# A fifth block product of the first layer, the fourth, taken by seven products of its own blocks

## The chip, the cores and the metric

The kernel runs on one core of one Trainium2 chip. The metric is the device time of one execution, in microseconds (us), as a median of several runs. All data are 32-bit floats.

## What is computed

Each of 4096 tokens of 512 numbers first passes a quaternion rotation (one 4x4 mixing of its four quarters of 128), then a mixture of 8 experts. Each token goes to the two experts that score highest, and an expert takes 1024 slots. Cut to what matters here, for expert e:

```python
h  = relu(de @ fc1_w[e].T + fc1_b[e])   # first layer:  1024 slots x 512 -> 2048
eo = h @ fc2_w[e] + fc2_b[e]            # second layer: 1024 slots x 2048 -> 512
out = x + sum(gates * eo[slot])         # rows go back to their tokens, weighted
```

## The kernel before, in words

TensorE (PE) does the matrix products into PSUM banks of 128 x 512 floats. VectorE (DVE) and ScalarE (ACT) read the banks and add into tiles of SBUF. GpSimd (POOL) forms the sums of weight blocks, gathers and scatters rows. SyncE (SP) issues the other transfers.

**Groups.** The work goes by 32 groups k = 4e + g: expert e, quarter g of its 2048 hidden units (512 of them). In a group each layer is a 2 x 2 by 2 x 2 block product, done with seven block products in place of eight (Strassen's method in Winograd's form); the sums of blocks that this needs are made by POOL for weights (`left1`, `right2`, `left_sub`, lines 110 to 162) and by POOL and DVE for inputs (`factors`, `right_sub`).

**First layer** (`layer1`, from line 842). One block product is 256 hidden units x 256 inputs x 512 slots. Taken whole, as `half` does it for products 0, 5 and 4, it is four matmuls of 128 x 512. Products 1, 6, 3 and 2 are instead taken by seven products of their own blocks (128 x 128 x 256 slots), each one matmul (`within`, line 831, which writes half a bank). Products 1 and 6 go together, as do 3 and 2 (`pair`, line 874): the left half of a bank is the term of the one and the right half that of the other, so a matmul pair (`both`) is followed by one DVE add that reads the whole bank (L888, L901, L907). Bank `t` accumulates term after term and is read in between; term 4 goes to another bank, `u`. The results are four tiles of 128 x 2 x 512: `h11`, `h21`, `r12`, which lie side by side in `beside`, and `h22`. Product 4 belongs to two of them: its value is added to `h21`'s running value to give `h22` (L925), and to `r12` (L917).

**Second layer** (`second_layers`). One of its units is a block product in four matmuls of 128 x 256 (`product2`, L796) and one add on DVE into the expert's accumulator (L1160, L1164, L1186, L1188, L1209, L1216, L1132).

**Each fp32 matmul is two instruction records on PE in the profile.** So a group has 112 records on L796, 24 of width 512 on L854 and 56 on L833.

**Order.** Two generators, first and second layer, are run in turn: one unit of the first, one unit of the second, 14 of each in a group; the first layer is two units ahead of the second's group. In between, `turn` takes steps from two lists: `background` (steps of rotating the next expert's rows on DVE and ACT, L723, L765, L767, the sums between layers of `chain`, and the stores) and `fetches` (gathers on POOL, exchanges on SP). The table `PACE` says how many steps follow each unit. `later` puts the sums of blocks after chosen units. The instructions of an engine run in the order in which they are written, and the framework sets the waits.

**PSUM.** `bank1` hands out four banks in rotation to the first layer: `a0`, `a1`, `t`, `u`, `b0`, `b1`, `t`, `u`. The second layer has three, the rotation one.

Of the kernel before, what the change touches and what calls it, by code (L numbers as in the profile page):

```python
# [39 lines left out]
P = 128  # L40
# [11 lines left out]
NG = 4  # L52
# [14 lines left out]
def kernel(  # L67
# [509 lines left out]
    hp = ctx.enter_context(tc.tile_pool(name="hp", bufs=1))  # L577
    vp = ctx.enter_context(tc.tile_pool(name="vp", bufs=3))
    xdp = ctx.enter_context(tc.tile_pool(name="xdp", bufs=2))
# [33 lines left out]

    beside = [hp.tile([P, 3, 2, HALF], F32, name=f"beside{i}") for i in range(2)]
    unused = [hp.tile([P, 2, HALF], F32, name=f"hidden{i}") for i in range(5)]

# [55 lines left out]
    class Slots:  # L672
# [36 lines left out]

        def arrivals(self, half):  # L710

            n = PER if half == 0 else 2
            t = self.a if half == 0 else self.b
            for at in range(0, PER, n):
                for st in range(n):
                    yield lambda st=st, at=at: self.gather_ahead(t[:, st], half, at + st)
                yield from [lambda: None] * 2
                for b in range(QT):
                    yield lambda b=b, at=at: self.exchange(t, half, at, b)
                yield from [lambda: None] * 2  # L720

# [70 lines left out]
    def product2(out, st0, factors, n, first, tiles=range(2)):  # L792

        for m in tiles:
            for c in range(2):
                nc.tensor.matmul(  # L796
                    out[m] if isinstance(out, list) else out[:, m],
                    lhsT=factors[0][n][:, c, (st0 + m) * P : (st0 + m + 1) * P],
                    rhs=factors[1][n][:, c, :],
                    start=first and c == 0 and (m == 0 or isinstance(out, list)),  # L800
                    stop=c == 1,
                    skip_group_check=True,
                )
        if st0 + 2 == PER and 1 in tiles and n in (2, 3, 4, 5):
            unused.append(factors[0][n])

    def chain(k, h22):


        h11, h21, r12 = (beside[k % 2][:, i] for i in range(3))  # L810
        s1, s2 = unused.pop(0), unused.pop(0)
        hidden[k] = [h11, h21, None, h22, s1, s2, r12]

        def last():
# [6 lines left out]
            lambda: V.scalar_tensor_tensor(r12, r12, 0.0, h11, ALU.max, ALU.subtract),  # L821
            *[lambda: None] * (2 if k == NK - 1 else 0),
            last,
        ]

    hidden = {}

    def relu(h):
        nc.scalar.activation(h, h, AF.Relu)  # L829
# [12 lines left out]
    def layer1(k, factors, subs):  # L842
# [4 lines left out]
        h = beside[k % 2]  # L847
        h11, h21, r12 = (h[:, i] for i in range(3))
        A, B = slice(0, HS), slice(HS, HALF)
# [23 lines left out]

        def pair(n, o, at, base, base_read):

            two = h[:, at : at + 2]
            t, u = bank1(f"t{n}_{k}"), bank1(f"u{n}_{k}")
            halves = t.rearrange("p (n s) -> p n s", n=2)  # L880

            def both(bank, i, first=False):
                within(bank[:, A], subs, n, i, first)
                within(bank[:, B], subs, o, i)

            def add(m, half):
                to = two[:, :, m, half]
                V.tensor_tensor(to, halves, to, ALU.add)  # L888

            within(base[:, A], subs, o, 1)  # L890
            within(base[:, B], subs, o, 2)
            base_read()
            both(t, 0, True)
            add(0, A)
            yield
            both(t, 5)
            add(0, B)
            both(u, 4, True)
            to = two[:, :, :, B]
            term = u.rearrange("p (n s) -> p n s", n=2).unsqueeze(2).to_broadcast([P, 2, 2, HS])  # L900
            V.tensor_tensor(to, term, to, ALU.add)  # L901
            yield
            both(t, 6)
            add(1, B)
            within(u[:, A], subs, n, 1, True)
            within(u[:, B], subs, n, 2)
            V.tensor_tensor(two[:, 0, 0], u, two[:, 0, 0], ALU.add)  # L907
            yield
            both(t, 3)
            add(1, A)  # L910
            relu(two[:, 0])

        def from5(m):
            nc.scalar.activation(h21[:, m], a[m], AF.Identity, bias=hi[:, m : m + 1])

        def from4(m):
            V.tensor_tensor(r12[:, m], b[m], r12[:, m], ALU.add)  # L917

        yield from pair(1, 6, 0, a[0], lambda: from5(0))
        yield  # L920
        h22 = unused.pop(0)
        b = [bank1(f"b{m}_{k}") for m in range(2)]
        for m in range(2):
            half(b[m], m, 4, True)
            V.tensor_tensor(h22[:, m], b[m], h21[:, m], ALU.add)  # L925
            if m == 1:
                from4(1)
                relu(h22)
            yield
        yield from pair(3, 2, 1, b[0], lambda: from4(0))  # L930
        chain(k, h22)
        yield

    PAIRS = (slice(0, 2 * P), slice(2 * P, 4 * P))

    def layer1_plain(k, w, x):
# [3 lines left out]

        h11, h21, r12 = (beside[k % 2][:, i] for i in range(3))
        h22 = unused.pop(0)
        for half in range(2):
# [6 lines left out]
            for at, i in ((at, i) for at in parts for i in range(NJ)):  # L950
# [22 lines left out]
                if half == 1 and done:  # L973
                    chain(k, h22)
                if len(parts) == 1 or i % 2:
                    yield

    def first_layers():
# [42 lines left out]
        lefts, right_subs = {}, {}  # L1021
        TURN_OF_SUM = {8: 2, 9: 0, 10: 1, 13: 3}
        nxt = None
        for k in range(NK):
            e, g = divmod(k, NG)
# [26 lines left out]
            if k:  # L1052
                for n, block, turns in (
                    (2, left_f[2], (2, 2, 3, 3)),
                    (3, w1_of[k][:, 1, 1], (4, 4, 5, 5)),
                ):
                    lefts[n], more = left_sub(k, n, block)
                    later(more, turns)
                if k == 1 or g == 0:
                    for n, turns in ((6, (1, 2, 2, 3)), (2, (4, 4, 5, 5)), (3, (6, 7, 8, 9))):  # L1060
                        right_subs[n], more = right_sub(xtp, e, n, xf[n])
                        later(more, turns)
# [6 lines left out]
            for i, _ in enumerate(units):  # L1069
# [3 lines left out]
                if k:  # L1073

                    if i == 8 and k + 1 < NK:
                        lefts[6], more = left_sub(k + 1, 6, left_n[6])
                        later(more, (9, 10, 11, 12))
                        lefts[1], more = left_sub(k + 1, 1, w1_of[k + 1][:, 0, 1])
                        later(more, (10, 11, 12, 13))
                        if g == NG - 1:  # L1080
                            right_subs[1], more = right_sub(xtp, e + 1, 1, xf_n[1])
                            later(more, (8, 9, 9, 12))
                    for f in ahead[i]:
                        f()
# [8 lines left out]
                if e + 1 < E:  # L1093

                    if (g, i) in ((0, 12 if e else 5), (1, 8)):
                        fetches.extend(nxt.arrivals(g))
                    if (g, i) in ((1, 11), (2, 9)):
                        background.extend(nxt.steps(g - 1))
# [21 lines left out]
    def second_layers():  # L1120
# [17 lines left out]
        for n, (k, st0) in enumerate(units):  # L1138
# [22 lines left out]
            yield  # L1161
            v2 = vp.tile([P, 2, DB], F32, tag="v", name=f"v2_{k}_{st0}")
            product2(a, st0, factors, 5, False)
            V.tensor_tensor(v2, a, i12, ALU.add)  # L1164
            yield
            tiles = STORED[2 * st0 : 2 * st0 + 4]
            last = n + 1 == len(units)
            if last:
# [4 lines left out]
                for m in range(2):  # L1173
                    r.weigh(tiles[m], o11[:, m], LEFT)
                    r.weigh(tiles[m], v2[:, m], RIGHT)
                    r.weigh(tiles[2 + m], i21[:, m], LEFT)
# [6 lines left out]
            yield  # L1183
            v3 = vp.tile([P, 2, DB], F32, tag="v", name=f"v3_{k}_{st0}")
            product2(a, st0, factors, 6, False)
            V.tensor_tensor(v3, a, i22, ALU.add)  # L1186
            for m in range(2) if last else [slice(0, 2)]:
                V.tensor_tensor(o22[:, m], b[m] if last else b, v3[:, m], ALU.add)  # L1188
            yield
# [25 lines left out]
            product2(b, st0, factors, 2, False)  # L1215
            V.tensor_tensor(o12, b, v2, ALU.add)  # L1216
            if last_of_group and k + 1 < NK:
# [12 lines left out]
    PACE = (  # L1230
        [(1, 1)] * 2 + [(0, 1)] * 4 + [(0, 0)] + [(0, 1)] * 5 + [(1, 1), (0, 0)],
        [(1, 1)] * 4 + [(1, 1), (0, 2), (0, 0), (0, 1), (1, 1)] + [(0, 1)] * 3 + [(1, 1), (0, 0)],
        [(1, 1)] * 2 + [(2, 1)] * 2 + [(1, 2), (0, 2), (0, 0), (0, 1), (1, 1)]
        + [(0, 1)] * 3 + [(1, 1), (0, 0)],
    )

    with tc.manual_schedule():
# [5 lines left out]
        while going:  # L1243
            going = False
            for n, gen in enumerate((first, second)):
# [3 lines left out]
                k, i = now  # L1249
                turn(1 if k in (0, NK - 1) else PACE[0 if k == 1 else min(k % NG, 2)][i][n])  # L1250
        while background:
# [46 lines left out]
```

## Time and profile before

| | |
|---|---|
| median of 3 runs | 1569.85 us (1569.73 to 1571.15) |
| the profiled execution's own time | 1569.29 us |
| its span, first to last instruction | 1567.4 us |
| PEld (weight loads), busy | 1190.9 us (76%) |
| ACT busy | 318.9 us (20%), 450 instructions |
| POOL busy | 1048.7 us (67%), 1133 instructions |
| granted TensorE clock | 0.987 on the mean |

The profile is one execution, seen by the hardware profiler. A row of groups gives line, engine, operation, tiles (output<-inputs), shape and count; then busy time and mean ns of one; then idle time of the engine before them, and what ended it. A row of the timeline gives start and length in us, then the same, and in brackets the idle time before it with its releaser. Matmul ends are modelled and overlap the next start, so the pace of PE is read from starts. In a group's 46.5 us in the middle of the run (700 to 746.5) PE is busy for 46.38 us, DVE for 39.00, ACT for 9.60 and POOL for 23.98.

### The profile page before, as it was taken

How to read it: one execution, taken by the hardware profiler on the slowest of the kernel's cores; microseconds unless marked ns; L12 is line 12 of the kernel's file. 1: busy time of each engine (PE TensorE's matmuls, PEld its weight loads, DVE VectorE, ACT ScalarE, POOL GpSimd, SP SyncE). 2: the span in 40 equal slices, each digit the busy share in tenths (PEclk: the TensorE clock that was granted, in tenths of full speed). 3: DMA queues.
4: the chain of work that ended last, by engine and by line, in shares of the span. 5: the costliest groups of instructions: out<-in, count | busy, mean ns of one | idle time of the engine just before them, and what ended most of it. 6: DMA issues, size and time to landing. Idle time of an engine off the chain costs nothing.

```text
span 1567.4 us, 17504 instructions
## 1 busy us (share of the span) xinstructions
PE 1529.9 (98%) x6399; PEld 1190.9 (76%) x6399; DVE 1152.7 (74%) x1601; ACT 318.9 (20%) x450; POOL 1048.7 (67%) x1133
## 2 busy tenths in 40 slices
PE   5899999999999999999999999999999999999996
PEld 3677877877777787777887777787787787777785
DVE  6568886588856887578875888758886688866665
ACT  3222112221122112222112221122113121221110
POOL 1754687746977477965779468775697747794535
PEclk7899999999999999999999999999999999999998
DMA  8463123511334103531135311342133420331003
GB/s 324 160 212 94 55 68 117 140 59 55 113 97 139 62 28 114 148 116 55 33 104 159 93 55 61 121 123 79 55 102 102 139 64 28 114 107 54 11 17 106
DMA packets 79373, 152.18 MB, mean 97 GB/s; under 512 B 12022, under 2 KB 40950, under 8 KB 74168
## 3 DMA queue, kind: packets, MB, share of 16 engines
q1 hardware_dynamic: 56848, 90.24, 18.7%
q0 software_dynamic: 18048, 52.31, 10.8%
q10 hardware_dynamic: 4392, 8.52, 1.4%
q8 instruction: 50, 0.82, 0.2%
q14 instruction: 35, 0.29, 0.1%
HBM read 119.77 MB, written 25.23 MB: 93 GB/s over the span
## 4 chain that ended last, share of the span: by engine, by line
PE 91%; DVE 4%; issue 2%; DMA 2%; POOL 1%; SPq 0%; POOLq 0%; DVEq 0%
PE a L796 26%; PE b L796 20%; PE t L833 14%; PE a L854 12%; PE u L833 7%; PE b L854 7%; PE p L955 2%; PE b L833 2%; PE a L833 1%; DMA xb<-in_xt_dram 1%; DVE hidden L820 1%; DVE xa L767 1%; POOL rows L601 0%; DVE hidden L816 0%; POOL out_dram L657 0%
## 5 line engine op out<-in xcount | busy, mean ns | idle before, releaser
L796 PE MATMUL a<-t,hidden 128*128 128x256 f32 x1024 | 244.0, 382 | 5.3 <-DVE v L1186 5.2
L796 PEld LDWEIGHTS a<-t,hidden 128*128 128x128 f32 x1024 | 195.9, 191 | 58.5 <-issue 27.5
L888 DVE TENSOR_TENSOR beside<-t,beside 128x512 f32<-128x512 f32 x248 | 170.3, 687 | 94.3 <-PE t L833 90.4
L829 ACT ACTIVATE beside<-beside 128x1024 f32<-128x1024 f32 x62 | 65.5, 1057 | 558.0 <-DVE beside L888 558.0
L833 PE MATMUL t<-xsub,sub 128*128 128x256 f32 x496 | 127.9, 380 | 0.4
L796 PEld LDWEIGHTS b<-w,hidden 128*128 128x128 f32 x504 | 96.0, 190 | 38.9 <-issue 29.1
L796 PE MATMUL b<-w,beside 128*128 128x256 f32 x512 | 121.1, 380 | 0.6 <-DVE acc L1209 0.6
L796 PE MATMUL a<-t,beside 128*128 128x256 f32 x512 | 121.0, 379 | 0.0
L796 PE MATMUL a<-w,beside 128*128 128x256 f32 x512 | 121.0, 379 | 0.0
L796 PE MATMUL b<-t,hidden 128*128 128x256 f32 x504 | 119.1, 379 | 0.0
L796 PE MATMUL b<-w,hidden 128*128 128x256 f32 x504 | 119.1, 379 | 0.0
L796 PEld LDWEIGHTS b<-w,beside 128*128 128x128 f32 x512 | 97.4, 190 | 27.1 <-issue 15.7
L796 PEld LDWEIGHTS a<-w,beside 128*128 128x128 f32 x512 | 97.5, 190 | 26.2 <-issue 14.8
L854 PE MATMUL b<-x,s 128*128 128x512 f32 x248 | 116.6, 593 | 0.0
L854 PE MATMUL a<-x,s 128*128 128x512 f32 x248 | 116.6, 593 | 0.0
L854 PE MATMUL a<-xa,w 128*128 128x512 f32 x248 | 116.4, 593 | 0.0
L137 POOL TENSOR_TENSOR s<-w 128x512 f32<-128x512 f32 x31 | 39.5, 1274 | 112.7 <-PE b L854 112.7
L139 POOL TENSOR_TENSOR s<-w 128x512 f32<-128x512 f32 x31 | 39.8, 1283 | 111.3 <-PE t L833 111.3
L140 POOL TENSOR_TENSOR s<-w,s 128x512 f32<-128x512 f32 x31 | 39.4, 1270 | 107.5 <-PE t L833 101.9
L796 PEld LDWEIGHTS a<-t,beside 128*128 128x128 f32 x512 | 97.4, 190 | 13.1
L796 PEld LDWEIGHTS b<-t,hidden 128*128 128x128 f32 x504 | 96.0, 190 | 12.8
L833 PEld LDWEIGHTS t<-xsub,sub 128*128 128x128 f32 x496 | 94.0, 190 | 14.6 <-DVE beside L888 2.3
(233 smaller groups left out, 3089.4 us busy)
## 6 DMA issues: line engine op xcount, KB each, us to landing
w<-in_w_dram SPq DMA_DIRECT2D x64, 1024.0 KB, 5.1
xb<-in_xt_dram SPq DMA_DIRECT2D x8, 1024.0 KB, 9.9
out_dram<-in_x_dram ACTq DMA_DIRECT2D x1, 8192.0 KB
rows<-xa SPq DMA_DIRECT2D x112, 64.0 KB, 2.1
rows<-xb SPq DMA_DIRECT2D x224, 32.0 KB, 1.9
b<-in_b_dram POOLq DMA_DIRECT2D x8, 256.0 KB, 3.8
c<-choice,slot_cho POOLq DMA_INDIRECT x64, 2.3
rows<-out_dram,slot_tok POOLq DMA_INDIRECT x64, 3.5
```

The source lines that it names most:

```text
L137: lambda: G.tensor_tensor(s[0], w[:, 1, 0], w[:, 1, 1], ALU.add),
L139: lambda: G.tensor_tensor(s[2], w[:, 0, 0], w[:, 1, 0], ALU.subtract),
L140: lambda: G.tensor_tensor(s[3], w[:, 0, 1], s[1], ALU.subtract),
L767: V.scalar_tensor_tensor(to, t, M[:, i, j : j + 1], to, ALU.mult, ALU.add)
L796: nc.tensor.matmul(out[m] if isinstance(out, list) else out[:, m], lhsT=factors[0][n][:, c, (st0 + m) * P : (st0 + m + 1) * P], rhs=factor ...
L820: lambda: V.tensor_tensor(s2, s1, h11, ALU.subtract),
L829: nc.scalar.activation(h, h, AF.Relu)
L833: nc.tensor.matmul(out, lhsT=subs[0][n][i], rhs=subs[1][n][i], start=first, stop=True, skip_group_check=True,)
L854: nc.tensor.matmul(out, lhsT=factors[0][n][:, c, m * P : (m + 1) * P], rhs=factors[1][n][:, c, :], start=first and c == 0, stop=c == 1, sk ...
L888: V.tensor_tensor(to, halves, to, ALU.add)
L955: nc.tensor.matmul(ps[n][m][:, at], lhsT=w[:, block, i // 2, i % 2, m * P : (m + 1) * P], rhs=x.of(half, i)[:, at], start=i == 0 and at.st ...
```

## The change

Product 4 of the first layer is taken by seven products of its own blocks, in all 31 groups that `layer1` does. Lines here are those of the changed kernel, where `within`'s matmul is L836.

- The two products without a sum of inputs, 1 and 2, go side by side into bank `b` (`singles`) and are added to `h21` for the first half of `h22` (L929); ACT copies `h21`'s second half to `h22` first (L925).
- The other five terms, 0, 5, 4, 6 and 3, go to one bank, `t4`: 0, 5, 6 and 3 accumulate in its left half, 4 is made in its right half. Each is added to both `h22` and `r12` by one DVE instruction, whose PSUM operand is repeated (`add_to_both`, L897; term 4 by L938).
- `h22` moves into `beside`, between `h11` and `h21`; the first layer's banks of a group are then `a0`, `a1`, `t`, `u`, `b`, `t4`, `t`, `u`.
- POOL forms four more sums of weight blocks a group (`left_sub` for 4), DVE four more of inputs an expert (`right_sub` for 4).
- The last sum of `chain` (s4) now waits in a list until product 2 of the group before has freed its tile. `v2` and `v3` of the second layer are gone: their adds write into the accumulator. The steps of gathering, exchanging, rotating and summing are placed after other units (`ARRIVE`, `PACE`, `later`).

The units of the first layer in a group stay 14. The core of the diff:

```diff
-    beside = [hp.tile([P, 3, 2, HALF], F32, name=f"beside{i}") for i in range(2)]
-    unused = [hp.tile([P, 2, HALF], F32, name=f"hidden{i}") for i in range(5)]
+    beside = [hp.tile([P, 4, 2, HALF], F32, name=f"beside{i}") for i in range(2)]
+    unused = [hp.tile([P, 2, HALF], F32, name=f"hidden{i}") for i in range(3)]
...
-        b = [bank1(f"b{m}_{k}") for m in range(2)]
-        for m in range(2):
-            half(b[m], m, 4, True)
-            V.tensor_tensor(h22[:, m], b[m], h21[:, m], ALU.add)
-            if m == 1:
-                from4(1)
-                relu(h22)
-            yield
-        yield from pair(3, 2, 1, b[0], lambda: from4(0))
-        chain(k, h22)
+        def add_to_both(two, m, half, term):
+
+            to = two[:, :, m, half]
+            V.tensor_tensor(to, term.unsqueeze(1).to_broadcast([P, 2, HS]), to, ALU.add)
...
+        nc.scalar.activation(h22[:, 1], h21[:, 1], AF.Copy)
+        two = h[:, 1:4:2]
+        b, t4 = bank1(f"b_{k}"), bank1(f"t4_{k}")
+        singles(b, 4, True)
+        V.tensor_tensor(h22[:, 0], b, h21[:, 0], ALU.add)
+        within(t4[:, A], subs, 4, 0, True)
+        add_to_both(two, 0, A, t4[:, A])
+        yield
+        within(t4[:, A], subs, 4, 5)
+        add_to_both(two, 0, B, t4[:, A])
+        within(t4[:, B], subs, 4, 4)
+        to = two[:, :, :, B]
+        term = t4[:, B].unsqueeze(1).unsqueeze(1).to_broadcast([P, 2, 2, HS])
+        V.tensor_tensor(to, term, to, ALU.add)
+        yield
+        three = h[:, 2:4]
+        t, u = bank1(f"t3_{k}"), bank1(f"u3_{k}")
+        singles(b, 2)
+        within(t4[:, A], subs, 4, 6)
+        add_to_both(two, 1, B, t4[:, A])
+        both(t, 3, 2, 0, True)
+        add_pair(r12, b)
+        add(three, 0, A, t)
+        yield
+        within(t4[:, A], subs, 4, 3)
+        add_to_both(two, 1, A, t4[:, A])
+        relu(h22)
+        both(t, 3, 2, 5)
...
                 for n, block, turns in (
-                    (2, left_f[2], (2, 2, 3, 3)),
-                    (3, w1_of[k][:, 1, 1], (4, 4, 5, 5)),
+                    (4, left_f[4], (2, 2, 3, 3)),
+                    (2, left_f[2], (4, 4, 5, 5)),
+                    (3, w1_of[k][:, 1, 1], (6, 6, 7, 7)),
                 ):
...
-                    for n, turns in ((6, (1, 2, 2, 3)), (2, (4, 4, 5, 5)), (3, (6, 7, 8, 9))):
+                    for n, turns in (
+                        (6, (2, 2, 3, 3)),
+                        (4, (3, 4, 4, 5)),
+                        (2, (5, 7, 7, 8)),
+                        (3, (8, 10, 10, 12)),
+                    ):
...
-            v2 = vp.tile([P, 2, DB], F32, tag="v", name=f"v2_{k}_{st0}")
             product2(a, st0, factors, 5, False)
-            V.tensor_tensor(v2, a, i12, ALU.add)
+            V.tensor_tensor(o12, a, i12, ALU.add)
```

`add` (L887), `add_twice` (L892) and `add_pair` (L900) are `pair`'s adds under names of their own. In the changed kernel the first add of the second layer's product 3 is L1266 (before: L1209), its start's L1191 (before: L1132).

## The prediction

> **What bounds the kernel now.** I read the page first, then the groups with shapes kept apart, then the timeline of two stretches. The page:
>
> ```profile
> span 1567.4 us, 17504 instructions
> ...
> PE 1529.9 (98%) x6399; PEld 1190.9 (76%) x6399; DVE 1152.7 (74%) x1601; ACT 318.9 (20%) x450; POOL 1048.7 (67%) x1133
> ...
> PE   5899999999999999999999999999999999999996
> ...
> PE 91%; DVE 4%; issue 2%; DMA 2%; POOL 1%; SPq 0%; POOLq 0%; DVEq 0%
> ```
>
> PE is full in all but the first and last slices and holds 91% of the chain that ended last. No other engine has to be waited for in between: what PE is spared comes off the time, and what PE is made to wait is added to it, whole. The groups say how full:
>
> ```profile
> L888 DVE TENSOR_TENSOR beside<-t,beside 128x512 f32<-128x512 f32 x248 | 170.3, 687 | 94.3 <-PE t L833 90.4 <-ACT beside L914 1.7
> L833 PE MATMUL t<-xsub,sub 128*128 128x256 f32 x496 | 127.9, 380 | 0.4
> ...
> L854 PE MATMUL b<-x,s 128*128 128x512 f32 x248 | 116.6, 593 | 0.0
> ...
> L901 DVE TENSOR_TENSOR beside<-u,beside 128x1024 f32<-128x1024 f32 x62 | 75.9, 1225 | 9.5 <-PE u L833 7.3
> ...
> L170 DVE TENSOR_TENSOR xsub<-x 128x256 f32<-128x256 f32 x16 | 14.2, 886 | 0.0
> ...
> L170 DVE TENSOR_TENSOR xsub<-xb 128x256 f32<-128x256 f32 x8 | 3.3, 415 | 0.0
> ```
>
> The matmuls have next to no idle time in front; DVE waits for PE, not the reverse. Means of matmuls overlap, so I take the pace from starts, in the timeline:
>
> ```profile
> 319.75 1.88 PE L854 MATMUL a<-x,s 128*128 128x512 f32 x4
> ...
> 321.46 1.89 PE L796 MATMUL b<-w,beside 128*128 128x256 f32 x8
> ...
> 323.00 2.06 DVE L767 SCALAR_TENSOR_TENSOR xa<-xps,M,xa 128x512 f32<-128x512 f32 x3
> ...
> 323.19 0.60 PE L833 MATMUL a<-x,s 128*128 128x256 f32 x2
> ...
> 324.92 1.89 PE L796 MATMUL a<-t,hidden 128*128 128x256 f32 x8
> ...
> 326.20 0.67 DVE L888 TENSOR_TENSOR beside<-t,beside 128x512 f32<-128x512 f32 x1
> ...
> 326.92 1.13 PE L833 MATMUL t<-xsub,sub 128*128 128x256 f32 x4
> ...
> 330.48 1.03 PE L833 MATMUL t<-xsub,sub 128*128 128x256 f32 x4
> ...
> 332.04 0.73 DVE L723 STREAM_TRANSPOSE xps<-rows 128x512 f32<-128x512 f32 x1
> ...
> 332.67 0.67 DVE L888 TENSOR_TENSOR beside<-t,beside 128x512 f32<-128x512 f32 x1
> ```
>
> and, near the end,
>
> ```profile
> 1542.43 1.89 PE L796 MATMUL a<-t,hidden 128*128 128x256 f32 x8
> ...
> 1542.63 0.69 DVE L1160 TENSOR_TENSOR acc<-b,v 128x512 f32<-128x512 f32 x1 [1.03 <-PE b L796]
> ```
>
> Four records of width 512 take 321.46 - 319.75 = 1.71, or 0.428 us each; eight of 256 take 323.19 - 321.46 = 1.73, or 0.216. A DVE add that has waited starts 0.20 us after PE has begun its next work (1542.63 against 1542.43) and takes 0.69. At 326.92 PE waited: the eight before it began at 324.92, so it was due at 326.65, and it began 0.05 after the add that reads `t` had ended (326.87). The four records then took 1.13, not the 1.03 of 330.48: a wait costs another 0.10 in starting again. On DVE work that lies ready follows at 0.63 after a transpose (332.67 - 332.04), 0.66 between the rotation's three ((2.06 - 0.74)/2, with 0.74 for one) and about 0.60 after an add of 512.
>
> **What is removed and added on PE.** In each of 31 groups product 4 loses four matmuls of 512 (eight records, 8 x 0.428 = 3.42 us) and gains seven of 256 (fourteen records, 14 x 0.216 = 3.02): 0.40 us a group, 12.5 us in all, if PE stays as dense. Taken alone that is 1556.8 by the profiled execution's own 1569.29.
>
> **The wait that is added.** In the unit after `t4` is begun, the lines stand thus: term 5 into `t4`'s left half, the add that reads the left half (L897), then term 4 into `t4`'s right half. In the built program this last matmul waits for the very DVE instruction that reads the left half: both halves are one bank, and the framework guards a bank, not columns. Between PE's write and PE's next instruction lies nothing else, so PE stands still for the whole way to DVE and back; behind the waiting matmul stand the next four of the second layer and all that follows. `pair` had its term 4 in another bank, `u`, and the only comparable trip in a group of before has a whole second-layer unit (1.73 us) under it. So before shows no such trip and its cost is built from rows. The rule that bears on it is in the Trainium skill, PSUM — Partial Sum Buffer, section PSUM bank collisions raise a hardware error: access by two engines has to be guarded by bank and quadrant of partitions, not by address, different columns colliding all the same. It speaks against the change. By addresses the two halves would not meet, and the sum would be -12.5; by the rule, which the built order follows, it is what comes now.
>
> Time zero is the start of term 5; term 4 was due at 0.43. On DVE the add of the second layer's preceding unit (L1266) stands ahead and starts at 0.20. Term 5 can be read from 0.43 + 0.20 = 0.63, but L897 comes 0.60 behind L1266, at 0.80, and ends at 1.49. PE resumes at 1.54: it lost 1.11, and 0.10 for starting again makes 1.21. With nothing ahead it would be 0.63 + 0.69 + 0.05 - 0.43 = 0.94.
>
> What else stands ahead of L897, by the built order of DVE:
> - groups 5, 9, ..., 29 and 30, 31: nothing. 9 x 1.21 = 10.9.
> - groups 2, 6, ..., 26: a transpose. 7 x (1.21 + 0.63) = 12.9.
> - groups 3, 7, ..., 27: a step of the rotation, and one sum of inputs before L1266 (0.42 by the row for `xb`, hidden, since DVE is through by about 3.2 us of the unit before, whose add is due at 3.22). 7 x (1.21 + 0.66) = 13.1.
> - groups 1, 4, 8, ..., 28: two sums of inputs before L1266. By the 415 ns row they are hidden; by the 886 ns row, which is that of the same tile kind (`x`), they end some 0.4 late. I take 0.4; 0 and 1.1 are the ends. 8 x 1.61 = 12.9.
>
> Sum 49.8 us of waits, less 12.5: +37.3.
>
> **What costs nothing, and by what cover.** DVE gets per group one add of 1024 (1.225) and two of 512 more (0.69 each), 2.6 us, and about 0.7 for the sums of inputs on the mean: 81 + 22 us, a load of some 1256 us in over 1600. It lies under PE, save where shown; without that cover its late adds would be more of the same wait. The closest other place is the first L897: it must end before term 5, 3.02 us into its unit, and by the sums above it ends at about 2.4 to 2.85; a margin of 0.2 to 0.6, cost 0 to 0.3 in the groups with rotation, 0 taken. POOL's four sums of weights a group (about 0.5 us each, 31 x 2.1 = 65 us) go into its idle third; their users come several units later. They move `left_sub` 2 and 3 back by two turns, and 1 and 6 forward by one to three; the stores, gathers and exchanges on POOL and SP are moved too, with several units of slack each: 0, at most 2 us either way. ACT's copy (0.69) goes into an engine that is 20% busy. `v2`, `v3`: the same adds, other target, 0. The later s4 sum has seven units before its product: 0. The four waits like that of 326.92 (together under 2 us) may go or stay.
>
> **The forecast.** 1569.29 + 37.3 = 1606.6; the median of the runs shown is 0.56 above that execution, so I say 1607. Its own range: without the 0.10 of starting again and the 0.4 of the sums it is 1600.6; with 1.1 for the sums and 0.3 at the first L897 in fourteen groups, 1617.
>
> **Rivals.**
> - *The saving lands* (4%): term 4's wait finds DVE done, the time is 1557. For it speaks that DVE is idle a quarter of the time; against it that 0.40 us a group is all there is to lose, and the shortest trip, with an idle DVE, is 0.94. From a wait of 0.40 us a group on this case turns slower; it is the one that ends on the other side.
> - *Only the bare trip* (6%): L1266 and the rotation don't delay L897, 31 x (0.94 + 0.10) - 12.5 = +20, 1589 to 1590. Against it: the built order has them ahead.
> - *The waits breed more* (10%): a longer wait of before, 5.16 us near the end, was followed by eight records at half pace (3.78 in place of 1.89 us). If each stop did that, 31 x 1.9 = 59 more, 1666. Against it: after the 0.27 us stop at 326.92 there is no such thing, and the Trainium skill (TensorE: Matmul & The Clock Gate, What's actually happening) gives an idle window of about 3.4 us for the gate, while the stops here are under 2. A smaller form, DVE late elsewhere too because sums of inputs meet POOL, gives 1617 to 1630.
>
> The main case has 80%; the range is 1599 to 1617. A difference under 0.2% (3.1 us) can't be told from none. Faster 0.04, same 0.01, slower 0.95.
>
> **What would show it.** Right: the idle time before PE's `t4` rows, ended by DVE L897, about 1.1 us each and up to 1.9 at the longest, 31 times; 0.432 us from start to start of a matmul of 256 elsewhere; PE's share of the span down to about 95%; DVE near 1256 us. Wrong: no idle before `t4` (then the first rival), or waits before other tiles of the first layer, or weight loads that wait for POOL. A granted clock below 0.95 would be the third rival.

## The result, and the profile after

The changed kernel takes 1655.39 us, median of 4 runs (1649.74 to 1661.19), against 1569.84 before: a ratio of 1.0543, 95% interval 1.0528 to 1.0557. The sign was as forecast, the size was not: +85.5 us where +37 was said, well above the 1599 to 1617 us of the range. The profiled execution is the longest of the four, 1661.19 us with a span of 1659.4; all sums below are against that one, 92.0 us of span more than before.

The page of the changed kernel, in the rows that were shown of before:

```profile
span 1659.4 us, 18188 instructions
...
PE 1550.2 (93%) x6585; PEld 1234.6 (74%) x6585; DVE 1258.7 (76%) x1726; ACT 334.9 (20%) x481; POOL 1119.0 (67%) x1257
...
PE 83%; DVE 10%; POOL 2%; DMA 2%; issue 2%; another core or an unknown queue 1%; SPq 1%; DVEq 0%; POOLq 0%
```

PE is no longer full (93%, before 98%), and DVE has 10% of the chain that ended last (before 4%). DVE's own load looks as forecast (1258.7 against 1256), but experiment 7 does the same 1726 instructions in 1218.3, so this agreement says little: DVE's busy time also holds what its instructions stood waiting. The groups of the changed kernel, shapes apart:

```profile
L836 PE MATMUL t<-xsub,sub 128*128 128x256 f32 x682 | 189.1, 389 | 60.3 <-DVE beside L897 60.3
L887 DVE TENSOR_TENSOR beside<-t,beside 128x512 f32<-128x512 f32 x248 | 170.6, 688 | 75.5 <-PE t L836 68.6 <-issue 3.6
...
L170 DVE TENSOR_TENSOR xsub<-xa 128x256 f32<-128x256 f32 x8 | 12.1, 1512 | 0.0
```

The first row is the forecast wait: 60.3 us of idle PE ahead of the terms, ended by L897; 12.6 of them are one stop in group 1, and 47.7 the others. In the last row a sum of 128x256, which takes 0.42 us where nothing is in its way, takes 1.51 on the mean. The waits of the changed kernel (engine, tile and line, what it waited for: total in us, times, longest) hold a second cause; in the kernel before no sum of inputs kept PE waiting:

```profile
PE t L836 <- DVE beside L897: 60.3, 33, 12.6
...
PE t L836 <- DVE xsub L173: 11.3, 5, 2.3
```

**Where the 92 us are.** As in the prediction, PE's pace is read from starts: whatever lies between two starts beyond 0.216 us (width 256) or 0.429 (512) is lost.

| | forecast, us | measured, us |
|---|---|---|
| work saved on PE | -12.5 | -12.4 (experiment 9) |
| 31 stops of term 4, with 0.10 each to start again | 49.8 | 55.8 |
| a stop of 12.8 in group 1 | 0 | 12.8 |
| five stops of 2.4 before term 3 of product 3, the last of its terms | 0 | 12.1 |
| records at half pace, 108 for 8 | 0 | 20.6 |
| small waits | 0 | 3 |

"Half pace" is a record of width 256 that takes 0.42 to 0.43 us from start to start in place of 0.216. The granted clock that goes with it is shown in the last section.

**A stop of the expected kind**, in group 5 of the changed kernel, by the timeline:

```profile
318.48 0.68 DVE L897 TENSOR_TENSOR beside<-t,beside 128x512 f32<-128x512 f32 x1
...
319.21 0.70 PE L836 MATMUL t<-xsub,sub 128*128 128x256 f32 x2 [0.91 <-DVE beside L897]
```

PE begins 0.05 us after L897 has ended, as the prediction reckoned, and loses 1.08 from start to start, or 1.18 with 0.10 for starting again (forecast 1.21).

**A stop of the unexpected kind**, in group 7, the last of an expert:

```profile
412.08 2.34 POOL L125 TENSOR_TENSOR x<-xc,xa 128x1024 f32<-128x1024 f32 x1
...
412.99 1.72 DVE L170 TENSOR_TENSOR xsub<-xa 128x256 f32<-128x256 f32 x1
...
414.63 0.68 DVE L1266 TENSOR_TENSOR acc<-a,acc 128x512 f32<-128x512 f32 x1
...
415.89 0.67 DVE L897 TENSOR_TENSOR beside<-t,beside 128x512 f32<-128x512 f32 x1
...
416.61 0.70 PE L836 MATMUL t<-xsub,sub 128*128 128x256 f32 x2 [2.79 <-DVE beside L897]
...
417.15 2.98 PE L796 MATMUL b<-w,hidden 128*128 128x256 f32 x8
```

L170 has both inputs in SBUF, and runs 1.72 us instead of 0.42, until POOL's L125 is through (414.42). The two steps behind it on DVE are then late, PE stands 2.79 us, and the eight records after that show 2.98 where eight take 1.89: half the pace for most of them.

This is not one case. In the changed kernel 84 of the 160 sums of inputs (L170 to L173) take more than 0.5 us, and every one of the 84 ends within 0.29 us of the end of a POOL operation. The 372 adds of the same kernel that take one operand from PSUM (L887, L897) stay at 0.66 to 0.69 us, though POOL is at work beside 279 of them. Overlap alone doesn't decide: 57 of the 76 quick sums have POOL work beside them too. The Trainium skill (SBUF — State Buffer, SBUF: two separate sides) has a rule for it: DVE and GpSimd share a pair of ports under an exclusive lock, taken for a whole instruction, and a DVE operation with two inputs in SBUF needs it against a GpSimd operation that reads SBUF. The traces agree with it.

The prediction had a row of slow sums (886 ns) beside one of quick ones (415), but not this reading of it, which the table of before already allowed. There 45 of 128 sums take more than 0.5 us and end in the same way, for instance

```profile
L173 DVE TENSOR_TENSOR xsub<-xa,xsub 128x256 f32<-128x256 f32 x8 | 12.1, 1517 | 0.0
```

but none stood where PE waits for it.

### The profile page after: what moved, and what is told of

Read it like the earlier page. It is cut to its first block, busy times and chain, and to the rows that moved or that the text cites. A ratio compares the mean times of both kernels' runs of the same rounds, so it can differ in the third digit from the quotient of the medians.

```text
span 1659.4 us, 18188 instructions
## 1 busy us (share of the span) xinstructions
PE 1550.2 (93%) x6585; PEld 1234.6 (74%) x6585; DVE 1258.7 (76%) x1726; ACT 334.9 (20%) x481; POOL 1119.0 (67%) x1257
## 4 chain that ended last, share of the span: by engine, by line
PE 83%; DVE 10%; POOL 2%; DMA 2%; issue 2%; another core or an unknown queue 1%; SPq 1%; DVEq 0%; POOLq 0%
PE a L796 23%; PE b L796 19%; PE t L836 16%; PE a L857 12%; PE u L836 6%; PE b L836 3%; DVE beside L897 2%; PE a L836 2%; DMA xb<-in_xt_dram 1%; DVE xsub L173 1%; DVE xsub L170 1%; DVE acc L1266 1%; DVE xb L767 1%; PE p L988 1%
## 5 line engine op out<-in xcount | busy, mean ns | idle before, releaser
L832 ACT ACTIVATE beside<-beside 128x1024 f32<-128x1024 f32 x93 | 98.3, 1057 | 797.1 <-DVE beside L887 521.6
L796 PE MATMUL a<-t,beside 128*128 128x256 f32 x1024 | 248.9, 387 | 5.3 <-DVE acc L1243 5.2
L836 PE MATMUL t<-xsub,sub 128*128 128x256 f32 x682 | 189.1, 389 | 60.3 <-DVE beside L897 60.3
L796 PEld LDWEIGHTS a<-t,beside 128*128 128x128 f32 x1024 | 199.3, 195 | 47.2 <-issue 13.4
L887 DVE TENSOR_TENSOR beside<-t,beside 128x512 f32<-128x512 f32 x248 | 170.6, 688 | 75.5 <-PE t L836 68.6
L836 PEld LDWEIGHTS t<-xsub,sub 128*128 128x128 f32 x682 | 126.0, 191 | 92.9 <-DVE beside L897 77.8
L137 POOL TENSOR_TENSOR s<-w 128x512 f32<-128x512 f32 x31 | 39.5, 1275 | 154.7 <-PE t L836 154.7
L796 PE MATMUL a<-t,hidden 128*128 128x256 f32 x512 | 121.0, 379 | 0.0
L796 PEld LDWEIGHTS b<-w,beside 128*128 128x128 f32 x512 | 97.1, 190 | 27.6 <-issue 15.3
L857 PE MATMUL a<-xa,w 128*128 128x512 f32 x248 | 116.4, 592 | 0.0
L796 PEld LDWEIGHTS a<-t,hidden 128*128 128x128 f32 x512 | 97.3, 190 | 13.2
L897 DVE TENSOR_TENSOR beside<-t,beside 128x512 f32<-128x512 f32 x124 | 84.8, 684 | 25.1 <-PE t L836 21.5
L669 POOL TENSOR_TENSOR rows<-acc,rows 128x512 f32<-128x512 f32 x60 | 76.9, 1282 | 21.1 <-ACT acc L667 20.6
```

The source lines that it names most:

```text
L137: lambda: G.tensor_tensor(s[0], w[:, 1, 0], w[:, 1, 1], ALU.add),
L669: nc.gpsimd.tensor_tensor(r, acc, r, ALU.add)
L796: nc.tensor.matmul(out[m] if isinstance(out, list) else out[:, m], lhsT=factors[0][n][:, c, (st0 + m) * P : (st0 + m + 1) * P], rhs=factor ...
L836: nc.tensor.matmul(out, lhsT=subs[0][n][i], rhs=subs[1][n][i], start=first, stop=True, skip_group_check=True,)
L857: nc.tensor.matmul(out, lhsT=factors[0][n][:, c, m * P : (m + 1) * P], rhs=factors[1][n][:, c, :], start=first and c == 0, stop=c == 1, sk ...
L887: V.tensor_tensor(to, bank.rearrange("p (n s) -> p n s", n=2), to, ALU.add)
```

## The experiments

Each kernel is the changed one with the edit shown. The kernel before ran on the same chips at 1570.4 to 1571.0 us.

**1. Term 4 to another bank.** Term 4 goes to the free half of `u`'s bank, which is allotted one unit earlier; every other instruction stays.

```diff
-        within(t4[:, B], subs, 4, 4)
+        t, u = bank1(f"t3_{k}"), bank1(f"u3_{k}")
+        within(u[:, B], subs, 4, 4, True)
...
-        term = t4[:, B].unsqueeze(1).unsqueeze(1).to_broadcast([P, 2, 2, HS])
+        term = u[:, B].unsqueeze(1).unsqueeze(1).to_broadcast([P, 2, 2, HS])
```

> Of the changed kernel, only the bank of product 4's term 4 is another: it is made in the right half of u, which lies free until two units later. Theory (the time over the forecast has four parts: waits of term 4 on its own bank 55 us, stops in group 1 for the rotation's rows 13 us, the fourth sum of xsub3 blocked by POOL 12 us, matmuls at half pace after stops of over 2 us 21 us): the waits of term 4 vanish with the half pace that follows those of groups 3, 7, ..., 27 (7 x some 8 records x 0.21 = 11 us), the other stops stay: 1655 - 55 - 11 = 1589, between 1580 and 1600. Rival (DVE is simply late, and the bank is only where it shows): PE waits for DVE at the next term in place of this one, and the time stays within 1% of 1655.

Measured: 1589.39 us, ratio 1.0121 (1.0104 to 1.0138). Of the 33 waits of PE for L897 one is left, the 11.6 us of group 1, and of 108 records at half pace 14. So the shared bank is what stops PE, and it bears most of the half pace too. That the time fell on the expected 1589 is in part luck: the five stops before term 3 of product 3, which were to stay, are gone as well, and 27 short waits for DVE of 0.3 to 0.8 us, 14 us together, are new. The other 18 us over the kernel before, 31 with the saving, are left without the shared bank.

**2. Product 4 whole, all moved steps kept.** Product 4 is taken by `half` in two units, as before the change; the sums, arrivals, rotation and `PACE` stay where the change put them.

```diff
-        singles(b, 4, True)
-        V.tensor_tensor(h22[:, 0], b, h21[:, 0], ALU.add)
-        within(t4[:, A], subs, 4, 0, True)
-        add_to_both(two, 0, A, t4[:, A])
...
+        half(b[0], 0, 4, True)
+        V.tensor_tensor(h22[:, 0], b[0], h21[:, 0], ALU.add)
+        yield
+        half(b[1], 1, 4, True)
+        V.tensor_tensor(h22[:, 1], b[1], h21[:, 1], ALU.add)
+        V.tensor_tensor(r12[:, 1], b[1], r12[:, 1], ALU.add)
```

> The changed kernel with product 4 taken whole again, as before; all its moves of steps, its fourth sets of sums (now unused) and its tiles stay. Theory: the moves alone cost the stop in group 1 (13), the blocked fourth sum of xsub3 (12) and the half pace after both (some 10): 1570 + 35 = 1605. Rival, the prediction's own claim that the moves cost nothing: 1568 to 1572.

Measured: 1596.73 us, ratio 1.0165 (1.0148 to 1.0182). With product 4 as before the moves cost 26 us, so the rival falls. The theory was 8 us too high, and its parts are not those measured: the stop in group 1 is 9.1 us, the last sum for product 3 holds PE only once, for 0.8, half pace adds under 2, and 14 us are short waits for DVE of 0.3 to 1.0 us that it didn't have.

**3. The rotation of the second expert's rows back to its place of before.**

```diff
-                    if (g, i) in ((1, 7), (2, 6)):
+                    if (g, i) in ((1, 7 if e else 11), (2, 6)):
...
+    FIRST = (
+        [(1, 1)] * 2 + [(2, 1)] * 2 + [(1, 2), (1, 2), (0, 0), (0, 1), (1, 1)]
+        + [(0, 1)] * 3 + [(1, 1), (0, 0)]
+    )
...
-                turn(1 if k in (0, NK - 1) else PACE[min(k % NG, 2)][i][n])
+                turn(1 if k in (0, NK - 1) else (FIRST if k in (2, 3) else PACE[0 if k == 1 else min(k % NG, 2)])[i][n])
```

> The changed kernel with the rotation of the second expert's rows begun in unit 11 of group 1, as before, not in unit 7, and the steps after units of groups 1 to 3 spread as before. Theory: the 12.6 us stop in group 1 goes, and the half pace after it (11 records x 0.21 = 2.3): 1655 - 15 = 1640. Rival: the rows land later still, or another step takes the stop's place: 1655 within 0.5%.

What the stop in group 1 of the changed kernel is, its timeline says:

```profile
92.75 23.65 SPq L703 DMA_DIRECT2D rows<-xa  x16
...
118.12 0.73 DVE L723 STREAM_TRANSPOSE xps<-rows 128x512 f32<-128x512 f32 x1 [12.39 <-DMA rows<-xa]
...
120.27 1.22 PE L836 MATMUL t<-xsub,sub 128*128 128x256 f32 x2 [12.63 <-DVE beside L897]
```

The rows are being handed out by SP until 116.4, and DVE, which had come to the transpose 12.4 us too early, could do nothing else meanwhile. The timeline of before has the same transfer at the same place:

```profile
92.66 23.39 SPq L703 DMA_DIRECT2D rows<-xa  x16
```

so the wait could have been read off ahead of time: the change begins the rotation four units earlier, at a moment when these rows were not there. Measured: 1647.82 us, ratio 1.0475 (1.0445 to 1.0504); 7.6 us won where 15 were expected. The 12.6 us stop is gone, but another comes 16 us later:

```profile
128.78 0.96 POOL L690 DMA_INDIRECT xb<-in_xq_dram,slot_tok  x1 [22.50 <-DMA rows<-xb]
...
135.89 1.94 PE L857 MATMUL a<-x,s 128*128 128x512 f32 x2 [3.31 <-POOL s L138]
```

Here it is POOL that stands for 22.5 us, at a gather that the change places after unit 9 of group 1 (`ARRIVE`) and that needs the exchange before it to be done; in the changed kernel POOL stands there as long (22.9), under PE's own stop. The weight sums queued behind it now come late for product 5. Undoing one of two moves that wait for the same transfers only passes the wait on to another engine.

**4. The sums of inputs for product 3 (tile `xsub3`) earlier.** In the changed kernel the last of them meets three POOL operations in a row; here in the first group of the third expert:

```profile
478.54 3.35 DVE L173 TENSOR_TENSOR xsub<-x,xsub 128x256 f32<-128x256 f32 x1
478.68 0.50 POOL L158 TENSOR_TENSOR sub<-s,sub 128x128 f32<-128x128 f32 x1
479.10 1.29 POOL L137 TENSOR_TENSOR s<-w 128x512 f32<-128x512 f32 x1
480.32 1.28 POOL L669 TENSOR_TENSOR rows<-acc,rows 128x512 f32<-128x512 f32 x1
...
481.95 0.70 PE L836 MATMUL t<-xsub,w 128*128 128x256 f32 x2 [2.32 <-DVE xsub L173]
```

```diff
-                        (3, (8, 10, 10, 12)),
+                        (3, (6, 6, 6, 8)),
```

> The changed kernel with the four sums of inputs for product 3 after units 6, 6, 6 and 8 in place of 8, 10, 10 and 12. Theory: five stops of 2.4 us before the last term of products 3 and 2 go, with the half pace after them (5 x some 8 x 0.21 = 8): 1655 - 20 = 1635. Rival: POOL's instructions hold the sums up wherever they stand, and the stop only moves: 1650 or more.

Measured: 1638.99 us, ratio 1.043 (1.0412 to 1.0447): 16.4 us won, near the 20 expected. All five stops are gone, and half-pace records fall from 108 to 68.

**5. The first sum of inputs for product 1 (tile `xsub1`) one unit later.** This is the sum L170 of group 7 shown above.

```diff
-                            later(more, (8, 10, 10, 12))
+                            later(more, (9, 10, 10, 12))
```

> As the changed kernel, with the first sum of xsub1 (L170) moved from unit 8 to unit 9 of the last group of an expert; the other three stay at 10, 10 and 12. In the changed kernel that sum was held 1.72 us by GpSimd's L125 just as DVE should have read product 4's term, and the stop of PE there was 2.95 us (7 groups), after which about eight matmuls ran at half pace. Theory (a stop's length decides whether half pace follows): the 7 stops fall to about 1.65 us, as in the other groups, and the half pace after them goes: 7 x (1.3 + 1.6) = 20 us less, about 1635 us, with some 50 half-pace records left of 108. Rival A (half pace follows the number of stops, or has another cause): only 7 x 1.3 = 9 us less, about 1646 us, and as many half-pace records as before. Rival B (the sum is held as long in unit 9 and delays a relu or product 3's reads there): no gain, 1650 to 1660 us.

Measured: 1636.03 us, ratio 1.0409 (1.0392 to 1.0427). By the timeline of this kernel, in group 3:

```profile
220.38 0.68 DVE L897 TENSOR_TENSOR beside<-t,beside 128x512 f32<-128x512 f32 x1
...
221.11 0.70 PE L836 MATMUL t<-xsub,sub 128*128 128x256 f32 x2 [1.53 <-DVE beside L897]
221.65 1.89 PE L796 MATMUL b<-w,hidden 128*128 128x256 f32 x8
```

The stop is 1.69 from start to start (2.95 in the changed kernel), and the eight records behind it take the full pace, 1.89. That holds in all seven groups. Rival A and rival B fall. Of the 38 records left at half pace, 10 follow the 13.2 us stop of group 1, 17 two of the five xsub3 stops (2.38 and 2.42), and 11 the 5.2 us stop near the end; the other three xsub3 stops (2.36 to 2.47) bring none.

**6. Own bank, and the second expert's arrivals and rotation of before.**

```diff
-                (0, 5): [(0, 0)],
-                (1, 0): [(0, 1)],
-                (1, 2): [(1, 0)],
-                (1, 5): [(1, 1)],
-                (1, 9): [(1, 2)],
-                (1, 12): [(1, 3)],
+                (0, 5): [(0, 0), None, (0, 1)],
+                (1, 8): [(1, 0), None, (1, 1), None, (1, 2), None, (1, 3)],
...
-                        fetches.extend(nxt.arrive(*part))
-                    if (g, i) in ((1, 7), (2, 6)):
+                        fetches.extend(nxt.arrive(*part) if part else [lambda: None] * 2)
+                    if (g, i) in ((1, 7), (2, 6)) if e else (g, i) in ((1, 11), (2, 6)):
```

with the edit of experiment 1 and the paces (`FIRST`) of 3.

> As the own-bank experiment (1589.4 us), and for the second expert's rows the fetching and the begin of the rotation are put back to their places of before: first part fetched and exchanged from unit 5 of group 0, second part from unit 8 of group 1, the rotation of the first part from unit 11 of group 1, with the paces of before in groups 1 to 3; the rotation of the second part still begins at unit 6 of group 2. Theory (the 11.7 us stop of group 1 and the half pace of about 3 us after it come only from DVE's transposition being ahead of the rows' transfer): 1589.4 - 15 = about 1574 us, with no PE wait over 1.5 us in groups 1 and 2. Rival (as when the rotation alone was put back, another late arrival takes the place: a GpSimd gather that waits for the exchange holds up the left sums): a stop of 3 us or more in group 1 or 2, and 1580 to 1586 us.

Measured: 1574.05 us, ratio 1.0024 (1.0014 to 1.0033), as the theory had it. PE has no stop over 0.15 us in groups 1 and 2.

**7. The same, with both sums moved as in 4 and 5.**

> As the kernel with its own bank and the second expert's arrivals of before (the run ahead of this one), and both DVE sums that GpSimd was seen to hold are moved: the xsub3 sums to units 6, 6, 6 and 8, the first xsub1 sum to unit 9. In the own-bank run the waits for DVE in the groups with these sums were 0.48 to 0.76 us in 13 places, and one of 0.29 us for xsub3. Theory (these waits are the lock with GpSimd): about 5 us less than that run, about 1569 us, level with the kernel before or a little under it, and PE's waits on t add up to under 5 us. Rival (the sums only meet other GpSimd work at their new places): no difference from that run, within 2 us, about 1574 us.

Measured: 1557.36 us, ratio 0.9914 (0.9898 to 0.9931). This version beats both kernels. It won 16.7 us on the run before, where 5 were expected, so the theory had the cause and a third of the size. Its page:

```profile
PE 1520.6 (98%) x6585; PEld 1223.2 (79%) x6585; DVE 1218.3 (78%) x1726; ACT 335.5 (22%) x481; POOL 1108.3 (71%) x1257
...
PE 94%; DMA 2%; POOL 1%; issue 1%; DVE 1%; SPq 0%; POOLq 0%; DVEq 0%
```

DVE does the same 1726 instructions in 46.7 us less than in experiment 6 (1265.0), POOL its 1257 in 13.2 less. Only 39 of DVE's instructions were moved; what they do is shift DVE and POOL against each other for a whole stretch. In experiment 6, at the end of group 4:

```profile
265.57 3.76 DVE L823 SCALAR_TENSOR_TENSOR hidden<-beside 128x1024 f32<-128x1024 f32 x1
265.73 1.29 POOL L138 TENSOR_TENSOR s<-s,w 128x512 f32<-128x512 f32 x1
...
266.96 1.28 POOL L669 TENSOR_TENSOR rows<-acc,rows 128x512 f32<-128x512 f32 x1
...
269.85 3.96 DVE L824 TENSOR_TENSOR hidden<-hidden,beside 128x1024 f32<-128x1024 f32 x1
```

and in experiment 7 at the same point:

```profile
264.50 1.22 DVE L823 SCALAR_TENSOR_TENSOR hidden<-beside 128x1024 f32<-128x1024 f32 x1
...
266.62 1.29 POOL L138 TENSOR_TENSOR s<-s,w 128x512 f32<-128x512 f32 x1
...
267.22 3.00 DVE L824 TENSOR_TENSOR hidden<-hidden,beside 128x1024 f32<-128x1024 f32 x1
```

L823 comes 1.07 us earlier and gets through before POOL's next sum. In experiment 6 PE lost 0.57 us in six such places, where the second layer's product 1 waited for a DVE add behind these two; in 7 it loses none.

**8. Only the first xsub1 sum moved**, on experiment 6.

> As the own-bank kernel with the arrivals of before (1574.1 us), with only the first xsub1 sum moved (unit 9 instead of 8), the xsub3 sums left at 8, 10, 10 and 12. It splits the 16.7 us that the two moves of sums brought together. What they removed was: PE's waits on t at 0.48 to 0.76 us in 13 places with their followers of 0.08 (8.8 us), 0.57 us in 6 places where product 2 waits for DVE behind L823 and L824 (3.5), 0.30 us in 6 places on u (1.8), and 1.2 of small ones. Theory (each sum costs what is seen at its own place: xsub1 those at the end of an expert's last group and the begin of the next, xsub3 those at the begin of the second group): 7 x (0.5 + 0.25 + 0.3) = 6 to 8 us less, about 1567 us. Rival (one of the two sums sets where DVE and GpSimd stand against each other for the rest, and the other has no part): either within 2 us of 1574, or within 2 us of 1557.

Measured: 1567.10 us, ratio 0.9978 (0.9969 to 0.9988). So xsub1 brings 7.0 of the 16.7 us when it is moved first, and xsub3 the other 9.7 on top; the other order was not run. The stops of 0.57 us stay (3.5 us), so these went with xsub3. That is the theory: each sum pays at its own place.

**9. Product 4 whole again, in the order of experiment 7.**

> As the kernel of the last run that was level with its PE work (own bank, arrivals and rotation of the second expert as before, xsub3 and xsub1 sums moved: 1557.4 us), with product 4 computed whole as before the change. It tells what the fifth product by seven is itself worth once nothing waits for it. Theory: PE's work is 12.6 us more (31 groups of eight half matmuls of 0.21 us, less the terms' own overhead), so about 1570 us, level with the kernel before. Rival A (the moves freed the path by themselves and the product by seven has no part in the gain): 1557 to 1560 us. Rival B (the whole product of 512 columns also frees DVE, and its waits with GpSimd): under 1566 us.

Measured: 1586.46 us, ratio 1.01 (1.0083 to 1.0117), 29.1 more than experiment 7; none of the three expectations holds. With product 4 whole the steps of DVE fall otherwise, and the sums of experiment 7 meet POOL again:

```profile
395.39 2.35 POOL L126 TENSOR_TENSOR x<-xb,x 128x1024 f32<-128x1024 f32 x1
...
395.80 2.23 DVE L171 TENSOR_TENSOR xsub<-xa,xsub 128x256 f32<-128x256 f32 x1
...
400.77 1.10 PE L836 MATMUL t<-xsub,sub 128*128 128x256 f32 x4 [0.98 <-DVE beside L887]
```

From starts, PE waits 15.0 us more here than in experiment 7 (7 x 1.14 at this place, 6 x 0.88 before the second layer's product 1, 7 x 0.30 before `u`, and small ones). The spans differ by 27.4 us, so 12.4 us are PE's work: the saving that was forecast as 12.5. A count of records says the same: 434 of width 256 more at 0.216 and 248 of width 512 fewer at 0.429 make 12.7 less in the changed kernel. A whole product 4 with the sums placed for its own order was not run; the kernel before is the nearest to it.

**10. Everything mended but the bank.** Experiment 7 with term 4 back in `t4`'s bank.

> The changed kernel with everything mended but the bank: the arrivals and the rotation of before, xsub3 and xsub1 sums moved; product 4's terms still use the one bank of their own that DVE reads while PE wants to write to it again. Against 1557.4 us with the terms in the right half of u's bank it gives the price of the one bank alone. Theory (stops per group as seen in the changed kernel, none over 1.7 us, so no half pace): 7 x 1.2 + 8 x 1.7 + 8 x 1.5 + 7 x 1.7 = 46 us, so about 1603 us, with the half-pace records near the 10 of a calm run. Rival A (stops of this length do bring half pace, and only the others hid it): 1603 + some 20 = over 1615 us. Rival B (with the other waits gone DVE reads the terms at once and the stops shrink): under 1590 us.

Measured: 1607.21 us, ratio 1.0233 (1.0216 to 1.025). The bank alone costs 49.9 us against experiment 7 (the prediction's sum was 49.8, the expectation here 46). Its 31 stops last 0.95 to 1.98 us, 47.9 together with 0.10 each to start again, and no record at half pace follows any of them: there are 7, all after the 5.2 us stop near the end. Rivals A and B fall. A forecast of +37.3 is what this kernel shows (+36.8).

## Why the prediction was right in sign and wrong in size

*The step that failed is "What costs nothing, and by what cover"*, and with it the dismissal of half pace. The forecast wait for the bank came as it was reckoned.

- *PE's saving, 12.5 us*: right, 12.4 by experiment 9; experiment 7 lies 13.2 below the kernel before. (31 x 0.40 is 12.4; and by its own terms the lower end of the range is 1600.9, not 1600.6. Nothing hangs on either.)
- *The wait for the bank*: the mechanism was right, and as a whole the size too (49.8 forecast, 49.9 by experiment 10, 47.9 of it in the stops themselves). In the changed kernel the classes, in the prediction's order, measured 10.6 us (forecast 10.9), 12.2 (12.9), 21.0 (13.1) and 12.0 (12.9), with 0.10 for starting again. Only the third was off, the last groups of the experts: mostly 2.95 us a stop where 1.77 was reckoned.
- *That third class failed at the words "hidden, since DVE is through by about 3.2 us of the unit before"*: the sum took 1.72 us, not 0.42, because POOL held it. The row for `xb` (415 ns) was the nearest by shape, not by what POOL does at that moment.
- *"What costs nothing" failed for the arrivals and for the sums.* "With several units of slack each: 0, at most 2 us either way" was said of gathers and exchanges, and the earlier begin of the rotation got no term at all: the stop in group 1 alone is 12.8 us, and with term 4 in a bank of its own the arrivals and the rotation cost 15.3 (experiment 6) and the sums 16.7 (experiment 7). "About 0.7 for the sums of inputs on the mean", said to lie "under PE, save where shown": the last xsub3 sum, at 3.35 us, cost 12.1 in five stops. One cover was a count of units, the other a mean load; neither new place was looked up. The transfer that the rotation waits for stood in the timeline of before. One of the signs named for being wrong did come: waits before other tiles of the first layer.
- *The third rival, half pace after stops, was given 10% and dismissed* since the stops would be under 2 us. The reasoning held where the stops were that short (experiment 10: none). It failed because two kinds of stop came out at 2.4 to 2.96, and 11 of those 12 brought some eight records at half pace, 20.6 us with those after group 1. So it was not a separate rival but a follower of the two sizes above. Its sign, a granted clock below 0.95, could not show it: 20.6 us of half pace left the mean at 0.971.
- *The first rival* (the saving lands, 1557) was rightly put low for this kernel; experiment 7 shows that it is what the change gives once term 4 has a bank that DVE isn't reading and the sums and arrivals keep clear of POOL and of late rows.

## What to carry to other kernels

A matmul into a bank that DVE is still reading costs a whole trip, here 0.95 to 1.98 us each time (experiment 10); the same term in a bank that lies idle cost nothing that could be seen (experiment 7), so give a term with a reader of its own to another bank before anything else is tuned. A step that is moved has to be checked at its new place, not by its engine's mean load: look in the timeline of before at when its data land, and, for DVE operations with both inputs in SBUF, at what POOL runs beside it. Where PE is the bound, the price of one late step is read in PE's pace behind it too: a stop that grew from 1.7 to 2.95 us mostly cost 1.7 more there.

## What the runs showed of the hardware

- *Half pace follows a stop by how much of it falls into one interval of a fixed grid.* The clock in the traces changes only on a grid of 3.413 us: in each of the twelve traces all pieces at half clock begin at whole multiples of that from each other, within 0.002 us. Counted from the span's start, the edges fall at 1.37 us in the trace of the changed kernel and at 0.98 in that of experiment 5 (and every 3.413 on). Two stops of the changed kernel before term 3 of product 3 are alike but for their place on it. The first, 2.39 us, ends at 878.60, and an interval ends at 878.59; the second, 2.41 us, ends at 1076.92, and an interval ends at 1076.57, so 2.06 lie on one side of the edge and 0.36 on the other. In the rows of each stop's interval and the next one (PEclk, the granted clock, is the figure before the last two):

```profile
core 0: us, PE busy (x) PEld busy (x) DVE busy (x) ACT busy (x) POOL busy (x), PEclk, DMA share, GB/s
875.18:878.59 3.41, 1.19 (x6) 0.71 (x4) 3.37 (x2) 0.00 (x0) 3.12 (x5) 1.00 0.20 77
878.59:882.01 3.42, 3.41 (x8) 2.79 (x9) 0.69 (x1) 0.57 (x1) 3.40 (x3) 0.50 0.22 81
1073.15:1076.57 3.42, 1.52 (x8) 0.99 (x6) 3.42 (x2) 0.00 (x0) 3.42 (x4) 1.00 0.21 78
1076.57:1079.98 3.41, 3.06 (x13) 2.58 (x14) 1.15 (x3) 1.06 (x1) 3.11 (x4) 1.00 0.20 77
```

- *All the stops of the twelve traces go by this.* Of the 189 stops of over 0.9 us (from 90 us on, at full clock, without the last 15 us), 33 had 2.2 us or more in one interval, and the clock was halved in the next one after all 33. 149 had under 1.97, and it was halved after none. Of the seven in between, three were followed by half clock and four were not. So one of 1.98 us could bring it (experiment 3), and one of 2.95 that an edge split into 1.14 and 1.81 did not (experiment 4). It is why 11 of the 12 stops of 2.36 to 2.96 us brought half pace in the changed kernel and 2 of 5 in experiment 5. One interval at half clock costs about 1.7 us: some eight records of 256 at 0.42 to 0.43 us.
- *The rule that the prediction leaned on.* The Trainium skill (TensorE: Matmul & The Clock Gate, What's actually happening) gives an idle window of about 3.4 us for it, and says that the window runs freely; the traces agree on its length and that it runs freely, and differ in that it needn't be idle throughout: 2.2 us of it were enough. With the edges falling differently from run to run it is likely, though only one of them has a trace, that the four runs of the changed kernel differ by it: 1649.74 us at a granted clock of 0.976, 1654.86 at 0.973, 1655.92 at 0.974, 1661.19 at 0.971.
- *A DVE sum can wait for several POOL operations.* The 128x256 sum that takes 0.42 us was held to 1.72 by one POOL operation of 2.34, and to 3.35 by three in a row; a 128x1024 one (L823) went from 1.22 to 3.76. Adds that read PSUM stayed at 0.66 to 0.69 beside the same kind of POOL work.
